# Convolution, Mamba and experts on one core: eight kept images, four pairs held in SBUF up to the loop, and pattern stores and constants at other places

## The chip, the cores and the metric

The kernel runs on one core of one Trainium2 chip. The metric is device time in microseconds (us): the median of three runs, each beginning to end of one execution. A profile of one more execution gives what each engine did and when. Engines are named as in the profile: PE (TensorE), DVE (VectorE), ACT (ScalarE), POOL (GpSimd); SP is the engine that issues most DMAs.

## The reference, cut to what matters

The input is 128 images of 128 channels and 16 x 16 pixels. Three layers follow one another, each added to its input:

```python
def conv_block(x):                      # gn(x) is a group norm over 32 groups
    h = act_quant(bn(x, gamma1, beta1))             # 4 bits
    out = conv3x3(h, weight_quant(w1) * pat1)       # cross pattern, 5 taps
    out = act_quant(bn(out, gamma2, beta2))
    return conv3x3(out, weight_quant(w2) * pat2) + x   # diagonal pattern, 5 taps
v = x + conv_block(gn(x))
t = v.transpose to tokens                           # 256 tokens an image, 128 wide
t = t + mamba(ln(t), fwd) + mamba(ln(t)[::-1], bwd)[::-1]
t = t + moe(ln(t))                                  # top 2 of 8 experts
```

One direction of mamba is a projection to z, x, B, C and dt; a causal convolution of width 4 with silu; softplus of dt; a scan in chunks of 64 tokens (products of decays inside a chunk, states between chunks); a gate silu(z), an RMS norm and a projection back. The layer norm ln is over the 128 channels of a token.

## The kernel before, in words

The images are taken two at a time: 64 pairs, each a tile of 128 channels x 512 pixels, or four tiles of 128 tokens x 128 channels once transposed.

**Setup (0 to 80 us).** SP loads all of x into 64 resident tiles xr (L370, 256 KB each), and behind it the weights of the later layers in 47 small loads (load_weights, L277) and the second convolution's weights w2 (L399). Meanwhile POOL builds two tiles r and c of patterns (L371 to L394), from which the loop makes its decay sums by a matmul; they are stored through POOL's own DMA queue to rows_d and cols_d in memory (L395, L396, 512 KB each). Statistics of each image are taken in four pieces, by DVE (L440) or, for each fourth image, ACT; normed (L417) turns them into a scale and a shift for each image, and into ares and bres (L427, L428), which the residual of the second convolution uses. bst is the table of statistics; one of its columns is set to zero piece by piece (L453). All this is in a pool named setup that is closed afterwards, so its bytes are used again by the first convolution.

**First convolution (80 to 163 us).** For each pair: q = x times scale plus bias on ACT or POOL (L520, L522; four buffers, L516), rounding into a padded image hpad on DVE (L191), five matmuls (L217), and a copy out of PSUM on ACT (L536), with statistics on DVE (L537). The result of the first six pairs stays in SBUF (kept, NKEPT, L559); that of the others is stored to memory (L539).

**Second convolution (169 to 284 us).** fetch (L578) loads a result back, ACT scales it (L582), DVE rounds it (L191), five matmuls; POOL or ACT scale the residual (L612, L610), and DVE adds it (L613). stored (of the pair before) transposes the result in four matmuls (L591), copies it out to a yt tile on ACT (L593, three buffers) and stores it to y_d (L594). At eight places second_weights does a step of work on the loop's weights, through the same two PSUM buffers "cm" as the transposes.

**Order.** Outside the loop the order on each engine is made by an automatic list scheduler: work comes in the order of the program, and work that is ready may go ahead on an engine that is idle. The loop is in a manual order: a table T gives for each step of each part a time within a period of 375 units, in which two pairs are done; the steps are sorted by it and issued so.

**The loop (284 us to the end).** part_a loads yt (for pairs 0 and 1 through POOL's queue, else SP, L713), takes the layer norm (L694 to L705: statistics and their combination on DVE, a power and two small operations on POOL, four scalings on ACT), transposes it on PE (L719) and copies it to uT on ACT (L722). part_c makes the decays for two pairs: dt_ps (L735), its copy dts (L741), a transpose (L743), dtr on DVE (L749), a chain of small DVE and ACT operations to daz (L785), sums r_ps on PE (L793), a store of the cumulative sums through SP (L809), which comes back as e (L953). x_ps (L846) and the rest follow. Before the loop starts, constants() loads three copies each of rows and cols, six loads of 512 KB on SP (L640, L641); in the table they stand after the second step of pair 1's part_a. The first steps of part_a for pairs 0 and 1 go ahead of everything else in the loop.

Of the kernel before, what the change touches and what calls it, by code (L numbers as in the profile page):

```python
# [26 lines left out]
BIG = 1e38  # L27
LNMIN = 2.0 ** -60
G = 4
NKEPT = 6  # L30


@with_exitstack
def kernel(ctx: ExitStack, tc: tile.TileContext, a: dict):
# [308 lines left out]
    with tc.tile_pool(name="w1p", bufs=1) as w1p:  # L343
# [15 lines left out]
        with tc.tile_pool(name="setup1", bufs=1) as setup, tc.tile_pool(  # L359
# [8 lines left out]

            for i in range(NP):
                nc.sync.dma_start(xr[i], x_c[:, 2 * i : 2 * i + 2, :])  # L370
            r = setup.tile([P, NH, 2, 2, P], BF16, name="r0")  # L371
            c = setup.tile([P, 2, 2, 2, 2, P], BF16, name="c0")
            far = setup.tile([HD, 1], BF16, name="far")
            nc.gpsimd.memset(far, -1e30)
            for h in range(NH):
                nc.gpsimd.tensor_copy(
                    r[:, h].rearrange("p d t l -> p (d t l)"), heads[:, h : h + 1].to_broadcast([P, 4 * P])
                )
                nc.gpsimd.tensor_copy(
                    r[0:HD, h].rearrange("p d t (f l) -> p (d t f) l", l=HD),  # L380
                    ident[0:HD, 0:HD].unsqueeze(1).to_broadcast([HD, 2 * 2 * 2, HD]),
                )
            for m in range(2):
                for d in range(2):
                    sign = 1 - 2 * d
                    nc.gpsimd.tensor_copy(
                        c[:, m, d].rearrange("p j f l -> p (j f l)"), triple[:, m : m + 1].to_broadcast([P, 4 * P])
                    )
                    for half in range(2):
                        nc.gpsimd.affine_select(  # L390
                            out=c[0:HD, m, d, :, half, :], in_=far.unsqueeze(2).to_broadcast([HD, 2, P]),
                            pattern=[[0, 2], [sign, P]], compare_op=ALU.is_ge, fill=0.0,
                            base=-sign * HD * half - 1, channel_multiplier=-sign,
                        )  # L394
            nc.gpsimd.dma_start(rows_d, r)  # L395
            nc.gpsimd.dma_start(cols_d, c)  # L396
            load_weights()
            w2 = w1p.tile([P, 9, P], F32, name="w2", tag="w")
            nc.sync.dma_start(w2, a["L0_conv_w2"])  # L399
# [1 line left out]

            bst = setup.tile([P, B, 6], F32, name="bst")
            junk = setup.tile([P, NT], F32, name="junk")

            def tb(name):
                return setup.tile([P, B], F32, name=name)
# [10 lines left out]
            def normed(c):  # L417

                of = slice(cuts[c], cuts[c + 1])
                var_, gm_, dev_, ga_, qv_, dm_ = (t[:, of] for t in (var, gm, dev, ga, qv, dm))  # L420
                nc.vector.reciprocal(ga_, ga_)
                nc.vector.tensor_tensor(dm_, ga_, ga_, ALU.mult)
                nc.vector.tensor_tensor(dm_, dm_, qv_, ALU.mult)
                nc.vector.tensor_scalar(dm_, dm_, -0.5, 1.5, ALU.mult, ALU.add)
                nc.vector.tensor_tensor(ga_, ga_, dm_, ALU.mult)
                nc.vector.scalar_tensor_tensor(shift[:, of], gm_, -1.0, ga_, ALU.mult, ALU.mult)
                nc.vector.tensor_scalar(ares[:, of], ga_, 1.0, SCALE, ALU.add, ALU.mult)  # L427
                nc.vector.tensor_scalar(bres[:, of], shift[:, of], SCALE, None, ALU.mult)  # L428
                nc.vector.tensor_tensor(dev_, dev_, ga_, ALU.mult)
                nc.vector.tensor_tensor(var_, var_, ga_, ALU.mult)  # L430
                nc.vector.tensor_tensor(var_, var_, ga_, ALU.mult)

            for c in range(4):
# [13 lines left out]
                if mine:  # L447

                    picked = slice(mine[0], cuts[c + 1], 4)
                    nc.vector.tensor_scalar(neg[:, picked], bst[:, picked, 1], -1.0 / NT, None, ALU.mult)  # L450
                    nc.vector.tensor_scalar(bst[:, picked, 1], neg[:, picked], -1.0, None, ALU.mult)
                    nc.vector.tensor_scalar(bst[:, picked, 4], neg[:, picked], -1.0, None, ALU.mult)
                    nc.gpsimd.memset(bst[:, picked, 5], 0.0)  # L453
# [29 lines left out]
                if c == 1:  # L483
                    for _ in weights:
                        pass
                if c == 3:
                    normed(c)

# [67 lines left out]
                nc.gpsimd.tensor_scalar(bi2, bet2, NLEV, tmp2, ALU.mult, ALU.add)  # L556


        kepts = ExitStack()  # L559
        keptp = kepts.enter_context(tc.tile_pool(name="keptp", bufs=1, side="right"))  # L560
        kept = {i: keptp.tile([P, 2, NT], F32, name=f"kept{i}") for i in range(min(NKEPT, NP // 4))}

        by_weights(how1, conv1, CROSS)

    def conv2(taps, nq):
        with tc.tile_pool(name="pc", bufs=6) as pc, tc.tile_pool(
# [18 lines left out]
            def stored(i):  # L585
                if i < 0:
                    return
                yt_ps = psw.tile([P, 512], F32, name=f"yt_ps{i}", tag="cm")
                flat = xr[i].rearrange("p b (j l) -> p (b j) l", l=P)
                for t in range(4):  # L590
                    nc.tensor.transpose(yt_ps[:, t * P : (t + 1) * P], flat[:, t, :], ident)  # L591
                yt = pc.tile([P, 4, P], F32, name=f"yt_{i}", tag="yt", bufs=3)
                nc.scalar.activation(yt.rearrange("p t c -> p (t c)"), yt_ps, AF.Copy, scale=1.0 / SCALE)  # L593
                nc.sync.dma_start(y_d[i], yt)  # L594

            for i in range(5):
                fetch(i)
# [2 lines left out]
            for i in range(NP):  # L600
# [12 lines left out]
                behind = nc.vector.scalar_tensor_tensor(xr[i], ps, less, xr[i], ALU.add, ALU.add)  # L613

                stored(i - 1)
                if i % max(NP // 8, 1) == max(NP // 8, 1) - 1:
                    with tc.issue_after(behind.ins):
                        next(weights, None)
            stored(NP - 1)
            for _ in weights:  # L620
                pass

# [39 lines left out]

    yts, uTs, xcs, xts, bcs, ccs, zs, ends_ = {}, {}, {}, {}, {}, {}, {}, {}
    table = ["none"]

    def act(out, in_, func, **more):
# [6 lines left out]

    gps, es, ygs, sqs, rrs, t2s, u2Ts, fps, gbs = {}, {}, {}, {}, {}, {}, {}, {}, {}

    latest = []

    def alone(made):  # L680
        latest[:] = [made.ins]

    def large(made):
        if latest:
            info = mybir.DependencyInfo(mybir.DependencyClass.Sync, mybir.DependencyReason.DATA)
            tc.add_manual_dep(made.ins, latest.pop().name, info, reason="keep apart")

    def layernorm(src, dst, nm):

        s6 = sm.tile([P, 4, 6], F32, name=f"s6{nm}", tag="s6")  # L690
        mv = sm.tile([P, 4, 2], F32, name=f"mv{nm}", tag="mv")
        rstd = sm.tile([P, 4], F32, name=f"rstd{nm}", tag="rstd")
        for t in range(4):
            nc.vector.bn_stats(s6[:, t, :], src[:, t, :])  # L694
        for t in range(4):
            nc.vector.bn_aggr(mv[:, t, :], s6[:, t, :])
        alone(nc.vector.tensor_scalar(rstd, mv[:, :, 1], EPS, None, ALU.add))
        yield
        nmr = sm.tile([P, 4], F32, name=f"nmr{nm}", tag="nmr")
        nc.gpsimd.tensor_tensor(rstd, rstd, mhalf[:, :4], ALU.pow)  # L700
        nc.gpsimd.tensor_tensor(nmr, mv[:, :, 0], rstd, ALU.mult)
        nc.gpsimd.tensor_scalar(nmr, nmr, -1.0, None, ALU.mult)
        yield
        for t in range(4):
            nc.scalar.activation(  # L705
                dst[:, t, :], src[:, t, :], AF.Identity, bias=nmr[:, t : t + 1], scale=rstd[:, t : t + 1]
            )
        yield

    def part_a(i):  # L710

        yt = yts[i] = pr.tile([P, 4, P], F32, name=f"yt{i}", tag="yt", bufs=6)
        (nc.gpsimd if i < 2 else nc.sync).dma_start(yt, y_d[i])  # L713
        yield
        u = pr.tile([P, 4, P], F32, name=f"u{i}", tag="u", bufs=2)
        yield from layernorm(yt, u, f"a{i}")
# [340 lines left out]
    def part_e(i):  # L1057

        u2 = pr.tile([P, 4, P], F32, name=f"u2{i}", tag="u", bufs=2)
        yield from layernorm(t2s[i], u2, f"b{i}")  # L1060
        u2_ps = bank4(f"u2_ps{i}", "o")
        for t in range(4):
            nc.tensor.transpose(u2_ps[:, t, :], u2[:, t, :], ident)  # L1063
# [193 lines left out]

# [28 lines left out]
```

## Time and profile before

| what | us |
|---|---|
| median of 3 runs | 2562.01 (2561.74 to 2562.10) |
| the profiled execution | 2561.65 |
| its span | 2559.9 |
| first matmul of the first convolution | 80.30 |
| first matmul of the second convolution | 168.66 |
| first statistics of the loop (DVE) | 284.08 |

The profiled execution's own time is 1.75 us longer than its span; the sums below are made against that execution. A line of the timeline reads: start, busy time, engine, line and operation, output and inputs by the program's names, shapes, how many instructions are taken together, and in brackets the idle time before the first of them with what ended it. A line of the waits reads: engine and what it waited to do, what it waited for, us in total, how often, the longest.

### The profile page before, as it was taken

Reading aid. Unit: us, or ns where it says so; the run is one execution under the profiler, and the core shown is the slowest. Engines: PE = TensorE matmul, PEld = TensorE weight load, DVE = VectorE, ACT = ScalarE, POOL = GpSimd, SP = SyncE. Lnnn points to the kernel's source line nnn. Section 1 sums busy time; section 2 is a strip of 40 time slices with the busy share of each in tenths; the row PEclk is TensorE's granted clock in tenths of the full one; section 3 lists DMA queues with packets and bytes.
Section 4 is the critical chain, followed back from the end, with each engine's and each line's share of the span. In section 5 each row is a group of like instructions: output and inputs, shape, how many; then the busy total and the mean of one; then the engine's idle time right before and its main releaser. Section 6 shows DMA issues by size and latency. Waiting matters only on the chain.

```text
span 2559.9 us, 49341 instructions
## 1 busy us (share of the span) xinstructions
PE 2420.2 (95%) x15940; PEld 1483.1 (58%) x15940; DVE 2251.0 (88%) x6171; ACT 2174.3 (85%) x4455; POOL 1631.6 (64%) x1692
## 2 busy tenths in 40 slices
PE   0788789999999999999999999999999999999997
PEld 0345355666666666666666666666666666666663
DVE  8887689999999999999999999999999999999883
ACT  5677599888998988889898888898988889898881
POOL 3577025666666667666666766666667666666666
PEclk9999799999999999999999999999999999999998
DMA  9468523334443433444444344433433444444343
GB/s 302 138 233 286 187 68 113 114 118 129 130 120 117 131 121 112 131 132 124 119 125 124 111 124 130 124 123 120 128 118 117 132 132 121 122 124 121 104 126 103
DMA packets 303767, 342.73 MB, mean 134 GB/s; under 512 B 56960, under 2 KB 226944, under 8 KB 303488
## 3 DMA queue, kind: packets, MB, share of 16 engines
q1 hardware_dynamic: 303040, 337.78, 43.1%
q8 instruction: 133, 2.18, 0.3%
q0 software_dynamic: 448, 1.57, 0.2%
q14 instruction: 146, 1.20, 0.2%
HBM read 264.30 MB, written 58.20 MB: 126 GB/s over the span
## 4 chain that ended last, share of the span: by engine, by line
PE 87%; DVE 5%; POOL 2%; ACT 2%; DMA 2%; issue 1%; SPq 0%; DVEq 0%; POOLq 0%; ACTq 0%
PE f_ps L1158 17%; PE x_ps L846 13%; PE y_ps L981 9%; PE z_ps L889 9%; PE o_ps L1041 9%; PE sg L934 5%; PE xt_ps L901 4%; PE y_ps L987 4%; PE g_ps L920 4%; PE cv L217 3%; POOL xr L612 2%; PE n_ps L1014 1%; PE u_ps L1063 1%; PE f_ps L1153 1%; PE u_ps L719 1%
## 5 line engine op out<-in xcount | busy, mean ns | idle before, releaser
L1146 POOL TENSOR_TENSOR gb<-gb,u2T 128x512 f32<-128x512 f32 x512 | 642.6, 1281 | 121.7 <-PE y_ps L987 70.9
L864 DVE SCALAR_TENSOR_TENSOR xc<-x_ps,cw,xc 128x510 f32<-128x510 f32 (+2 forms) x768 | 571.3, 744 | 47.4 <-ACT xc L858 37.8
L997 POOL TENSOR_TENSOR yg<-yg,z 128x512 f32<-128x512 f32 x256 | 326.4, 1280 | 351.0 <-DVE yg L993 155.1
L1158 PE MATMUL f_ps<-gb,ew 128*128 128x512 f32 x1024 | 511.6, 603 | 6.0 <-POOL gb L1146 5.8
L846 PE MATMUL x_ps<-uT,wx 128*128 128x512 f32 x768 | 401.1, 604 | 9.7 <-ACT e L674 3.3
L674 ACT ACTIVATE e<-sg 128x512 f32<-128x512 f32 x512 | 299.6, 592 | 49.7 <-PE sg L934 44.4
L674 ACT ACTIVATE e<-e,ends 128x128 f32<-128x128 f32 x1024 | 324.9, 392 | 0.0
L981 PE MATMUL y_ps<-e,xt 128*64 128x256 f32 x2048 | 317.7, 389 | 0.1
L962 DVE TENSOR_TENSOR e<-e,g_ps 128x1024 f32<-128x1024 f32 x256 | 311.4, 1216 | 5.8 <-ACT e L674 2.7
L864 DVE SCALAR_TENSOR_TENSOR bc<-x_ps,cw,bc 128x510 f32<-128x510 f32 (+2 forms) x384 | 286.6, 746 | 20.5 <-ACT bc L858 4.8
L1158 PEld LDWEIGHTS f_ps<-gb,ew 128*128 128x128 f32 x1024 | 181.2, 192 | 173.5 <-issue 137.2
L889 PE MATMUL z_ps<-uT,wz 128*128 128x512 f32 x512 | 272.2, 613 | 1.6 <-issue 0.8
L858 ACT ACTIVATE xc<-x_ps,cb,cw 128x512 f32<-128x512 f32 x256 | 199.1, 778 | 63.6 <-PE x_ps L846 57.2
L1041 PE MATMUL o_ps<-wo,yg 128*128 128x128 f32 x2048 | 251.3, 276 | 0.2 <-DVE e L967 0.2
L1041 PEld LDWEIGHTS o_ps<-wo,yg 128*128 128x128 f32 x2048 | 240.4, 193 | 11.1 <-DVE g L1118 8.4
L993 DVE SCALAR_TENSOR_TENSOR yg<-xc,dcol,y_ps 128x512 f32<-128x512 f32 x256 | 189.5, 741 | 50.4 <-PE y_ps L987 47.0
L1029 POOL TENSOR_TENSOR rr<-rr,mhalf 128x8 f32<-128x8 f32 x64 | 110.0, 1719 | 161.5 <-DVE g L1120 82.3
L987 PE MATMUL y_ps<-e,xt 128*64 128x128 f32 x2048 | 198.9, 273 | 0.0
L934 PE MATMUL sg<-rows,cols 128*128 128x256 bf16 x1024 | 192.1, 274 | 5.8 <-ACT e L674 2.9
L987 PEld LDWEIGHTS y_ps<-e,xt 128*64 128x64 f32 x2048 | 146.9, 137 | 74.2 <-DVE e L967 0.5
L981 PEld LDWEIGHTS y_ps<-e,xt 128*64 128x64 f32 x2048 | 118.9, 136 | 100.8 <-issue 53.8
L967 DVE TENSOR_TENSOR e<-e,g_ps 128x512 f32<-128x512 f32 x256 | 174.0, 680 | 0.0
(256 smaller groups left out, 4802.0 us busy)
## 6 DMA issues: line engine op xcount, KB each, us to landing
gb<-gd SPq DMA_DIRECT2D x256, 512.0 KB
e<-cum SPq DMA_DIRECT2D x256, 256.0 KB
xr<-in_x SPq DMA_DIRECT2D x64, 256.0 KB
y<-yt SPq DMA_DIRECT2D x64, 256.0 KB
cc<-bc SPq DMA_DIRECT2D x128, 128.0 KB
out<-ob SPq DMA_DIRECT2D x64, 256.0 KB
yt<-y SPq DMA_DIRECT2D x62, 256.0 KB
o<-o SPq DMA_DIRECT2D x58, 256.0 KB
```

What stands on the lines that cost most here:

```text
L674: nc.scalar.activation(out, in_, func, **more)
L846: nc.tensor.matmul(ps, wx[d][:, n * P : (n + 1) * P], uTs[i], start=True, stop=True)
L864: nc.vector.scalar_tensor_tensor(acc[:, :, to], raw[:, :, of], cw[:, d, n, 3 - back : 4 - back], acc[:, :, to], ALU.mult, ALU.add,)
L889: nc.tensor.matmul(ps, wz[:, d, n * P : (n + 1) * P], uTs[i], start=True, stop=True)
L934: nc.tensor.matmul(sg[:, :, of], c_[:, k, d, s, half, :], r_[:, :, d, s, of], start=True, stop=True)
L962: nc.vector.tensor_tensor(e0.rearrange("p h t l -> p h (t l)"), e0.rearrange("p h t l -> p h (t l)"), gps[i, d, k][:, 0:NT].unsqueeze(1).t ...
L981: nc.tensor.matmul(y_ps[64 * q : 64 * q + 64, k, :], xt[:, 2 * k + s0, 64 * h : 64 * h + 64], e0[:, h].rearrange("p t l -> p (t l)"), star ...
L987: nc.tensor.matmul(y_ps[64 * q : 64 * q + 64, k, s1 * P : (s1 + 1) * P], xt[:, 2 * k + s1, 64 * h : 64 * h + 64], e1[:, h, :], start=False ...
L997: large(nc.gpsimd.tensor_tensor(yg, yg, zs[i, d][:, n, :], ALU.mult))
L1041: nc.tensor.matmul(o_ps[:, (2 * j + d) * P : (2 * j + d + 1) * P], ygs[i, d, n][:, t * P : (t + 1) * P], wo[d][:, n, :], start=(n == 0), s ...
L1146: large(nc.gpsimd.tensor_tensor(gb[:, e], gb[:, e], u2Ts[i], ALU.mult))
L1158: nc.tensor.matmul(f_ps, ew[:, e, :], gbs[i, e], start=False, stop=(e == NE - 1))
```

## The change

Eight results of the first convolution stay in SBUF and not six. A new pool, first, lives from before the first convolution to the end of the kernel: it holds yt of pairs 0 to 3 and uT of pairs 0 and 1. The second convolution writes those yt tiles there and doesn't store them, and the loop doesn't load them. For pairs 0 and 1 the layer norm, the transposes and the copy to uT are done inside the second convolution, in five steps each, one step after each pair from pair 32 on (early); in the loop their part_a has empty steps. The function layernorm is moved up and takes the pool as an argument, with its body as before. In setup, the building of the pattern tiles is a function called after the first convolution's weights, and the two stores of them are on SP's queue, emitted after load_weights and w2. The zero column of bst is set once. ares and bres are computed on POOL and not on DVE. The constants are loaded ahead of the loop's first step. No DMA is left on POOL's queue, and the memory set aside for such DMAs (dynamic_dma_scratch_size) is made smaller. What is cut below is marked; the body of patterns() is the loop that is removed, with the tiles' new names.

```diff
@@ constants @@
-NKEPT = 6
+NKEPT = 8
+NFIRST = 4
@@ setup, pattern tiles @@
-            r = setup.tile([P, NH, 2, 2, P], BF16, name="r0")
-            c = setup.tile([P, 2, 2, 2, 2, P], BF16, name="c0")
+            rows0 = setup.tile([P, NH, 2, 2, P], BF16, name="rows0")
+            cols0 = setup.tile([P, 2, 2, 2, 2, P], BF16, name="cols0")
             far = setup.tile([HD, 1], BF16, name="far")
-            nc.gpsimd.memset(far, -1e30)
-            for h in range(NH):
...
-            nc.gpsimd.dma_start(rows_d, r)
-            nc.gpsimd.dma_start(cols_d, c)
+            def patterns():
+                nc.gpsimd.memset(far, -1e30)
+                for h in range(NH):
...
             load_weights()
             w2 = w1p.tile([P, 9, P], F32, name="w2", tag="w")
             nc.sync.dma_start(w2, a["L0_conv_w2"])
@@ setup, statistics @@
+            nc.gpsimd.memset(bst[:, :, 5], 0.0)
...
-                nc.vector.tensor_scalar(ares[:, of], ga_, 1.0, SCALE, ALU.add, ALU.mult)
-                nc.vector.tensor_scalar(bres[:, of], shift[:, of], SCALE, None, ALU.mult)
+                nc.gpsimd.tensor_scalar(ares[:, of], ga_, 1.0, SCALE, ALU.add, ALU.mult)
+                nc.gpsimd.tensor_scalar(bres[:, of], shift[:, of], SCALE, None, ALU.mult)
...
-                    nc.gpsimd.memset(bst[:, picked, 5], 0.0)
...
                 if c == 1:
                     for _ in weights:
                         pass
+                    patterns()
+                    nc.sync.dma_start(rows_d, rows0)
+                    nc.sync.dma_start(cols_d, cols0)
@@ before the first convolution @@
+        first = ctx.enter_context(tc.tile_pool(name="first", bufs=1, side="right"))
+        yts = {i: first.tile([P, 4, P], F32, name=f"yt{i}") for i in range(NFIRST)}
+        uTs = {i: first.tile([P, 4 * P], F32, name=f"uT{i}") for i in range(2)}
@@ second convolution @@
-                yt = pc.tile([P, 4, P], F32, name=f"yt_{i}", tag="yt", bufs=3)
+                yt = yts[i] if i in yts else pc.tile([P, 4, P], F32, name=f"yt_{i}", tag="yt", bufs=3)
                 nc.scalar.activation(yt.rearrange("p t c -> p (t c)"), yt_ps, AF.Copy, scale=1.0 / SCALE)
-                nc.sync.dma_start(y_d[i], yt)
+                if i not in yts:
+                    nc.sync.dma_start(y_d[i], yt)
+
+            def early(i):
+                u = pc.tile([P, 4, P], F32, name=f"u{i}", tag="yt", bufs=3)
+                yield from layernorm(pc, yts[i], u, f"a{i}")
+                u_ps = psw.tile([P, 512], F32, name=f"u_ps{i}", tag="cm")
+                for t in range(4):
+                    nc.tensor.transpose(u_ps[:, t * P : (t + 1) * P], u[:, t, :], ident)
+                yield
+                nc.scalar.copy(uTs[i], u_ps)
+                yield
+
+            early_steps = [step for i in range(2) for step in [early(i)] * 5]
...
                 stored(i - 1)
+                if i >= NP // 2 and early_steps:
+                    next(early_steps.pop(0))
...
             stored(NP - 1)
+            for step in early_steps:
+                next(step)
@@ loop @@
-        yt = yts[i] = pr.tile([P, 4, P], F32, name=f"yt{i}", tag="yt", bufs=6)
-        (nc.gpsimd if i < 2 else nc.sync).dma_start(yt, y_d[i])
-        yield
+        if i >= NFIRST:
+            yts[i] = pr.tile([P, 4, P], F32, name=f"yt{i}", tag="yt", bufs=6)
+            nc.sync.dma_start(yts[i], y_d[i])
+        yield
+        if i < 2:
+            for _ in range(5):
+                yield
+            return
...
-        first = [n for n, (t, *_) in enumerate(steps) if t in [places[0] for places in T["a",]]]
-        for n in first:
-            next(steps[n][2])
-        for n, (t, _, stream) in enumerate(steps):
-            if n not in first:
-                next(stream)
-            if t == T["a",][1][1] and t < PERIOD:
-                constants()
+        constants()
+        for _, _, stream in steps:
+            next(stream)
@@ launch @@
-    nc = bacc.Bacc("TRN2", target_bir_lowering=False, num_devices=1)
+    nc = bacc.Bacc("TRN2", target_bir_lowering=False, num_devices=1, dynamic_dma_scratch_size=1024)
```

More of the change, by code (lines that the diff above doesn't have):

```diff
@@ L370 @@
                 nc.sync.dma_start(xr[i], x_c[:, 2 * i : 2 * i + 2, :])
-            r = setup.tile([P, NH, 2, 2, P], BF16, name="r0")
-            c = setup.tile([P, 2, 2, 2, 2, P], BF16, name="c0")
+            rows0 = setup.tile([P, NH, 2, 2, P], BF16, name="rows0")
+            cols0 = setup.tile([P, 2, 2, 2, 2, P], BF16, name="cols0")
             far = setup.tile([HD, 1], BF16, name="far")
-            nc.gpsimd.memset(far, -1e30)
-            for h in range(NH):
[L376 to L382, printed above, removed]
@@ L383 @@
-            for m in range(2):
-                for d in range(2):
-                    sign = 1 - 2 * d
+            def patterns():
+                nc.gpsimd.memset(far, -1e30)
+                for h in range(NH):
                     nc.gpsimd.tensor_copy(
-                        c[:, m, d].rearrange("p j f l -> p (j f l)"), triple[:, m : m + 1].to_broadcast([P, 4 * P])
+                        rows0[:, h].rearrange("p d t l -> p (d t l)"), heads[:, h : h + 1].to_broadcast([P, 4 * P])
                     )
[L389 to L393, printed above, removed]
-                        )
@@ L395 @@
-            nc.gpsimd.dma_start(rows_d, r)
-            nc.gpsimd.dma_start(cols_d, c)
+                    nc.gpsimd.tensor_copy(
+                        rows0[0:HD, h].rearrange("p d t (f l) -> p (d t f) l", l=HD),
+                        ident[0:HD, 0:HD].unsqueeze(1).to_broadcast([HD, 2 * 2 * 2, HD]),
+                    )
+                for m in range(2):
+                    for d in range(2):
+                        sign = 1 - 2 * d
+                        nc.gpsimd.tensor_copy(
+                            cols0[:, m, d].rearrange("p j f l -> p (j f l)"), triple[:, m : m + 1].to_broadcast([P, 4 * P])
+                        )
+                        for half in range(2):
+                            nc.gpsimd.affine_select(
+                                out=cols0[0:HD, m, d, :, half, :], in_=far.unsqueeze(2).to_broadcast([HD, 2, P]),
+                                pattern=[[0, 2], [sign, P]], compare_op=ALU.is_ge, fill=0.0,
+                                base=-sign * HD * half - 1, channel_multiplier=-sign,
+                            )
@@ L563, with alone, large, layernorm @@
         by_weights(how1, conv1, CROSS)
+    latest = []
+    def alone(made):
+        latest[:] = [made.ins]
+    def large(made):
+        if latest:
+            info = mybir.DependencyInfo(mybir.DependencyClass.Sync, mybir.DependencyReason.DATA)
+            tc.add_manual_dep(made.ins, latest.pop().name, info, reason="keep apart")
+    def layernorm(pool, src, dst, nm):
+        s6 = pool.tile([P, 4, 6], F32, name=f"s6{nm}", tag="s6")
+        mv = pool.tile([P, 4, 2], F32, name=f"mv{nm}", tag="mv")
+        rstd = pool.tile([P, 4], F32, name=f"rstd{nm}", tag="rstd")
+        for t in range(4):
+            nc.vector.bn_stats(s6[:, t, :], src[:, t, :])
+        for t in range(4):
+            nc.vector.bn_aggr(mv[:, t, :], s6[:, t, :])
+        alone(nc.vector.tensor_scalar(rstd, mv[:, :, 1], EPS, None, ALU.add))
+        yield
+        nmr = pool.tile([P, 4], F32, name=f"nmr{nm}", tag="nmr")
+        nc.gpsimd.tensor_tensor(rstd, rstd, mhalf[:, :4], ALU.pow)
+        nc.gpsimd.tensor_tensor(nmr, mv[:, :, 0], rstd, ALU.mult)
+        nc.gpsimd.tensor_scalar(nmr, nmr, -1.0, None, ALU.mult)
+        yield
+        for t in range(4):
+            nc.scalar.activation(
+                dst[:, t, :], src[:, t, :], AF.Identity, bias=nmr[:, t : t + 1], scale=rstd[:, t : t + 1]
+            )
+        yield
     def conv2(taps, nq):
@@ L591, in stored @@
                     nc.tensor.transpose(yt_ps[:, t * P : (t + 1) * P], flat[:, t, :], ident)
-                yt = pc.tile([P, 4, P], F32, name=f"yt_{i}", tag="yt", bufs=3)
+                yt = yts[i] if i in yts else pc.tile([P, 4, P], F32, name=f"yt_{i}", tag="yt", bufs=3)
                 nc.scalar.activation(yt.rearrange("p t c -> p (t c)"), yt_ps, AF.Copy, scale=1.0 / SCALE)
-                nc.sync.dma_start(y_d[i], yt)
+                if i not in yts:
[4 more added lines that the diff above has]
+                u_ps = psw.tile([P, 512], F32, name=f"u_ps{i}", tag="cm")
+                for t in range(4):
+                    nc.tensor.transpose(u_ps[:, t * P : (t + 1) * P], u[:, t, :], ident)
+                yield
+                nc.scalar.copy(uTs[i], u_ps)
+                yield
+            early_steps = [step for i in range(2) for step in [early(i)] * 5]
             for i in range(5):
@@ L661 @@
     NR = NTL * NH * 2
-    yts, uTs, xcs, xts, bcs, ccs, zs, ends_ = {}, {}, {}, {}, {}, {}, {}, {}
+    xcs, xts, bcs, ccs, zs, ends_ = {}, {}, {}, {}, {}, {}
     table = ["none"]
@@ L676, with part_a @@
     gps, es, ygs, sqs, rrs, t2s, u2Ts, fps, gbs = {}, {}, {}, {}, {}, {}, {}, {}, {}
[L678 to L697, printed above, removed]
-        yield
[L699 to L702, printed above, removed]
-        yield
[L704 to L710, printed above, removed]
-        yt = yts[i] = pr.tile([P, 4, P], F32, name=f"yt{i}", tag="yt", bufs=6)
-        (nc.gpsimd if i < 2 else nc.sync).dma_start(yt, y_d[i])
-        yield
+    def part_a(i):
+        if i >= NFIRST:
+            yts[i] = pr.tile([P, 4, P], F32, name=f"yt{i}", tag="yt", bufs=6)
+            nc.sync.dma_start(yts[i], y_d[i])
+        yield
+        if i < 2:
+            for _ in range(5):
+                yield
+            return
         u = pr.tile([P, 4, P], F32, name=f"u{i}", tag="u", bufs=2)
-        yield from layernorm(yt, u, f"a{i}")
+        yield from layernorm(sm, yts[i], u, f"a{i}")
         u_ps = bank4(f"u_ps{i}", "o")
@@ L1059, in part_e @@
         u2 = pr.tile([P, 4, P], F32, name=f"u2{i}", tag="u", bufs=2)
-        yield from layernorm(t2s[i], u2, f"b{i}")
+        yield from layernorm(sm, t2s[i], u2, f"b{i}")
         u2_ps = bank4(f"u2_ps{i}", "o")
```

## The prediction

> **What bounds the kernel now.** I read the page first (busy times, chain of waits), then the timeline at the three places that the change touches: the start of the first convolution, the second convolution, the start of the loop.
>
> ```profile
> span 2559.9 us, 49341 instructions
> PE 2420.2 (95%) x15940; PEld 1483.1 (58%) x15940; DVE 2251.0 (88%) x6171; ACT 2174.3 (85%) x4455; POOL 1631.6 (64%) x1692
> PE 87%; DVE 5%; POOL 2%; ACT 2%; DMA 2%; issue 1%; SPq 0%; DVEq 0%; POOLq 0%; ACTq 0%
> ```
>
> PE is the bound over the whole: 95% busy, 87% of the chain. The idle 5%, some 140 us, lies mostly before the steady loop: setup to 80.3 us, a gap at 162 to 169, a thin start of the loop. The change adds matmuls nowhere and removes none (eight transposes move). So it can only shorten or lengthen those thin places; the loop is issued in a fixed order and PE is full in it from about 350 us, so what its start gains should stay.
>
> Timeline of the start of the first convolution:
>
> ```profile
> 17.94 0.77 POOL L395 DMA_DIRECT2D rows_d<-r  x1
> 19.82 0.56 POOL L396 DMA_DIRECT2D cols_d<-c  x1 [0.17 <-POOL bst L453]
> ...
> 76.48 3.06 ACT L520 ACTIVATE q<-xr,bi,sc 128x256 f32<-128x256 f32 x6 [5.74 <-DVE bi L506]
> 80.30 3.15 PE L217 MATMUL cv<-hpad,wq 128*128 128x512 bf16 x7 [5.94 <-DVE hpad L191]
> 82.37 0.39 SPq L399 DMA_DIRECT2D w<-in_L_conv_w  x1
> ```
>
> The reader sees three facts: the pattern tiles leave SBUF at 18 to 20 us; SP is still issuing weight loads at 82 us, two us after the convolution began; and the convolution waits for DVE's coefficients.
>
> Timeline of the loop's start:
>
> ```profile
> 284.08 0.81 DVE L694 BATCH_NORM_STATS2 s6a<-yt 128x6 f32<-128x128 f32 x4
> 287.16 3.25 ACT L705 ACTIVATE u<-yt,nmra,rstda 128x128 f32<-128x128 f32 x8 [2.24 <-POOL nmra L702]
> 288.58 1.30 SPq L713 DMA_DIRECT2D yt<-y  x2
> 290.93 1.34 PE L735 MATMUL dt_ps<-uT,wdt 128*32 128x128 f32 x16
> 296.78 0.87 DVE L694 BATCH_NORM_STATS2 s6a<-yt 128x6 f32<-128x128 f32 x4 [10.16 <-DMA yt<-y]
> 298.12 0.41 DVE L749 TENSOR_TENSOR dtr<-dt_ps,dtb 128x16 f32<-128x16 f32 x4
> 302.07 1.22 PE L793 MATMUL r_ps<-sums,daz 128*128 128x128 f32 x4 [7.23 <-DVE daz L785]
> ```
>
> L749 heads the chain that releases r_ps, and stands behind pair 2's statistics on DVE, which wait 10.16 us for a load that SP issued behind six constant loads. PE waits 7.23 us for the end of that.
>
> The waits between 165 and 284 us:
>
> ```profile
> DVE xr L613 <- PE cv L217: 19.9, 37, 2.0
> ACT q L582 <- DMA q<-o: 16.2, 18, 1.6
> DVE xr L613 <- POOL xr L612: 5.4, 9, 1.8
> ```
>
> In the second convolution PE and DMA share the bound: 115.5 us for 64 pairs (1.80 each) against 1.54 us of matmul and transposes, at 0.85 DMA share and 285 GB/s.
>
> **What the Trainium skill says.** "DMA: Bandwidth & Descriptors", section "Issuing engines are not separate DMA queues": DMAs of all engines run on the same 16 DMA engines and interleave. The trace agrees: the x loads and the two pattern stores together move some 350 GB/s between 10 and 55 us. "SBUF — State Buffer", section "SBUF: two separate sides": a port pair of DVE and GpSimd is locked for a whole instruction. The trace agrees: a DVE operation of 128x128 (L354) takes 4.44 us from 13.63, and ends at 18.07, 0.08 after POOL's pattern burst at 17.99; a similar one (L81) takes 0.27 when POOL is quiet.
>
> **Loop start: -11.6 us.** Pairs 0 to 3 need no load and pairs 0 and 1 come with uT made. The last transposes of the convolution end at 284.24. dt_ps needs only uT, so it can start at 284.3 in place of 290.93. It takes 0.65 (its later row for 16), the copy to dts ends 0.6 after that, and L743 0.47 later: 286.2. On DVE the memsets L647 end at 284.16; pair 2's statistics, now from SBUF, take 0.81+0.36+0.17 = 1.35 and end by 285.5. L749 then starts at about 286.5, not 298.12: 11.6 earlier. What comes after is late next: the small DVE and ACT steps to daz, 3.9 us as before, all released by L749. The constants now stand first on SP: 3.1 MB at 285.4, at 350 GB/s till about 294.4. The cum store (305.56 before) would be due at 293.9, behind them on the same queue, and costs up to 3 us of delay; its reader e is first needed near 319-11.6, so I cost it at nothing. Without that cover it is 1 to 3 us. Bounds: -8 (constants delay the loop) to -13 (PE's clock, 0.66 granted in 280 to 310, recovers earlier).
>
> **First convolution: +6.0 us.** This is the hidden step. The pattern stores move from POOL's queue at 18 us to SP, where they are emitted behind 64 x loads, the 47 weight loads and w2. SP issues in order. Before, w2 went out at 82.37; the x loads end 3.0 us earlier (1.05 MB of stores no longer among them, at 350 GB/s), so w2 goes at 79.4 and the stores at 80.0 and 80.6. Who waits for them: the first convolution's q buffers (L516) take the place of the setup's closed pool. In the compiled program of before, r lies at bytes 197024 to 201120 of a partition, c at 201120 to 205216, the four q buffers between 197056 and 205248; the first L520 waits for the rows_d store to be complete, and the second pair's for cols_d's. Before, both were met at about 26 us, 50 us ahead of need; after, they are the last to come. Landing: w2 0.59 MB and the store 0.52 MB at 350 GB/s, 3.2 us, and some 2 us fixed, my estimate from the trace: its cum store of 32 KB shows 2.25 us from issue to the load that waits for it. So rows_d is complete at 84.5 to 85. ACT's 0.51 x 2 and DVE's 0.43, with issue gaps, put the first matmul 1.7 later: 86.5 in place of 80.30. Queued behind L520 on ACT are the other q's; POOL's L522 waits likewise. I take +6.0; bounds +4.5 (smaller loads drain faster) and +7.5. That weight loads stood behind x before too is the same in both.
>
> **Setup's engines: 0.** Memsets merged, ares and bres on POOL (8 DVE operations of about 0.1 to 0.2 less), the patterns perhaps built later so that DVE's stalls of 4.2+1.3 us go: all of it makes bi1 earlier by 0 to 5 us, but the hold above ends later than bi1 (76.45), so it is worth nothing while that stands. If the hold is gone, it is 0 to -5. Where the patterns are built later, the same lock may stall DVE there; that too is covered by the hold, up to 6 us.
>
> **Second convolution: 0.** Removed: four y stores (1.05 MB) here, two kept images' store and fetch (0.52 MB each way; the store belongs to the first convolution). At 285 GB/s that is up to 5 us of transfer, but only 16.2 us of ACT's waits over 18 fetches come from DMA, and only two fetches of 58 go: -0.6 by share, -2 at best. Added for pairs 0 and 1: PE 8 x 0.27 = 2.2, DVE 2 x 1.35, ACT 2 x (4 x 0.41 + 0.58) = 4.4, POOL 2 x 1.5 = 3.0. PE idles some 9 us of 110 there, ACT is busy 84 of 110, DVE 77, POOL 70: they fit beside the transfers, except PE's, of which part is paid. The chain has waits: u waits for POOL's pow, u's transposes take a "cm" buffer of two that the y transposes use, and u takes one of three "yt" buffers. Net 0, bounds -3 and +4.
>
> **Sum.** -11.6 + 6.0 + 0 + 0 = -5.6. Against the profiled execution, 2561.65 (span 2559.9 and 1.75 around it): 2556.0. The median of the runs, 2562.01, is 0.36 above it, so 2556.4 there; I write 2556.
>
> **Rivals.**
> B, no hold: the stores go out early on SP (the order of issue outside the loop is made by a scheduler, which could put them among the x loads), or q's addresses are freed otherwise. For it: they are ready early if POOL builds the patterns at once. Against: SP's queue is emitted in that order. Then -11.6 and 0 to -5 of setup: 2545 to 2550, say 2548.
> D, the second convolution gains more than I allow, or the hold is nearer 4: -10, 2552. For it: DMA share of 0.85. Against: PE's waits there are short, 2 us at most.
> C, slower: the early layer norm stalls ACT in the second convolution. POOL runs ahead through L612 from 170.78 at 0.617 each; if pair 0's pow stands behind 59 of them, it comes at 207.2, and nmr at 208.8. If ACT reaches u at about 198.4, it stands 10.4 us, with all later q's behind it, so hpad and PE wait. With both pairs' chains conv2 grows by 8 to 12: total +2.4 to +6.4, 2566 in the middle. It ends slower from 5.6 us of stall on. Against: u's buffer follows pair 31's yt, which ACT makes at about 226, long after POOL's pow.
>
> **Chances.** About 0.2%, 5.1 us, is what a measurement here can tell from no change. A (forecast, 2553 to 2559) 0.55: it straddles -5.1, so 0.31 faster, 0.24 same. B 0.17 and D 0.13, faster. C 0.15: 0.10 slower, 0.05 same. Together 0.61, 0.29, 0.10. The range 2546 to 2565 leaves out a third of B and half of C, 0.13.
>
> **What would show it.** Hold: the pattern stores on SP's queue after w2 at about 80, and ACT's first q waiting for them, first matmul at 86 to 87. Wrong if it is at 80 or earlier. Loop start: L749 within 2 to 3 us of the last transposes and no wait for yt. Conv2: first to last matmul still 115 to 116 us; C if ACT's u shows a long wait for POOL.

## The result, and the profile after

The changed kernel takes 2557.66 us, the median of 20 runs (2554.65 to 2561.57); the kernel before, in 20 runs beside them, 2562.29 (2559.89 to 2566.29). The ratio is 0.9981, with a 95% interval of 0.9974 to 0.9988: 4.6 us less, by the medians. The profiled execution of the changed kernel took 2554.94 us and has a span of 2553.1, so it lies at the fast end of its runs, 6.7 below the profiled execution of before (6.8 by the spans).

The views here and below show the lines that matter; lines between them are left out. The page of the changed kernel: span, busy times, and the chain that ended last by engine.

```profile
span 2553.1 us, 49290 instructions
PE 2415.3 (95%) x15940; PEld 1479.9 (58%) x15940; DVE 2253.2 (88%) x6163; ACT 2173.0 (85%) x4455; POOL 1629.3 (64%) x1694
PE 88%; DMA 4%; DVE 3%; ACT 2%; issue 1%; SPq 1%; POOL 1%; POOLq 0%; ACTq 0%; DVEq 0%
```

PE has as many matmuls as before and is as busy. What has changed is in the small shares: DMA is 4% of the chain in place of 2%, and DVE 3% in place of 5%. Two percent are some 50 us, far more than the change can have cost: it is the path through setup that is another. Before, the chain up to the first matmul went in large part through DVE's statistics; now it goes through the loads of x, SP's issuing of the weight loads one after the other, and the landing of a pattern store. The timeline of the changed kernel from 79 us on shows where the two paths meet.

```profile
79.03 0.67 SPq L401 DMA_DIRECT2D w<-in_L_conv_w  x1
79.74 0.43 SPq L489 DMA_DIRECT2D rows_d<-rows  x1
80.21 0.43 SPq L490 DMA_DIRECT2D cols_d<-cols  x1
85.72 3.23 ACT L525 ACTIVATE q<-xr,bi,sc 128x256 f32<-128x256 f32 x6 [13.64 <-DMA rows_d<-rows]
85.75 0.16 DVE L211 TENSOR_SCALAR less<-less_ps 128x1 f32<-128x1 f32 x1 [8.13 <-DMA rows_d<-rows]
87.06 7.28 POOL L527 TENSOR_SCALAR q<-xr,sc,bi 128x256 f32<-128x256 f32 x11 [10.59 <-DMA cols_d<-cols]
87.33 12.85 PE L218 MATMUL cv<-hpad,wq 128*128 128x512 bf16 x47 [11.41 <-DVE hpad L192]
```

The reader sees the hold of the prediction's second step: the pattern stores are the last of SP's queue, ACT's first q waits for the first of them to land, POOL's for the second, and the first matmul is at 87.33 and not at 80.30.

The loop's start in the changed kernel, from its timeline:

```profile
292.12 0.86 DVE L589 BATCH_NORM_STATS2 s6a<-yt 128x6 f32<-128x128 f32 x4
292.91 0.65 PE L766 MATMUL dt_ps<-uT,wdt 128*32 128x128 f32 x16
293.61 1.04 POOL L595 TENSOR_TENSOR rstda<-rstda,mhalf 128x4 f32<-128x4 f32 x1 [44.83 <-issue]
294.31 0.42 DVE L780 TENSOR_TENSOR dtr<-dt_ps,dtb 128x16 f32<-128x16 f32 x4
298.44 0.71 PE L824 MATMUL r_ps<-sums,daz 128*128 128x128 f32 x4 [3.31 <-DVE daz L816]
```

dt_ps (290.93 before, under L735) follows the last transposes of the convolution at once, and pair 2's statistics need no load. The wait of 10.16 us for a load is gone.

From each trace I took when certain instructions start; the differences of these, stage by stage, add up to what the profiled execution gained in span. A group of transposes counts from the start of its last one.

| stage | before | after | difference | predicted |
|---|---|---|---|---|
| to the first matmul of the first convolution | 80.3 | 87.3 | +7.0 | +6.0 |
| from there to the first matmul of the second | 88.4 | 87.4 | -1.0 | 0 |
| from there to the last group of transposes | 115.3 | 118.0 | +2.7 | 0 (-3 to +4) |
| from there to dtr | 14.15 | 1.60 | -12.55 | -11.6 |
| from dtr to the 25th x_ps | 52.3 | 50.9 | -1.4 | in the bound of -13 |
| from there to the last o_ps | 2167.76 | 2167.76 | 0.0 | 0 |
| to the end | 41.7 | 40.1 | -1.6 | 0 |

### The profile page after: what moved, and what is told of

It reads as the page before. It is cut to its first block, busy times and chain, and to the rows that moved or that the text cites. A ratio compares the mean times of both kernels' runs of the same rounds, so it can differ in the third digit from the quotient of the medians.

```text
span 2553.1 us, 49290 instructions
## 1 busy us (share of the span) xinstructions
PE 2415.3 (95%) x15940; PEld 1479.9 (58%) x15940; DVE 2253.2 (88%) x6163; ACT 2173.0 (85%) x4455; POOL 1629.3 (64%) x1694
## 4 chain that ended last, share of the span: by engine, by line
PE 88%; DMA 4%; DVE 3%; ACT 2%; issue 1%; SPq 1%; POOL 1%; POOLq 0%; ACTq 0%; DVEq 0%
PE f_ps L1189 17%; PE x_ps L877 13%; PE y_ps L1012 10%; PE z_ps L920 9%; PE o_ps L1072 9%; PE sg L965 5%; PE xt_ps L932 4%; PE y_ps L1018 4%; PE g_ps L951 4%; PE cv L218 4%; DMA xr<-in_x 2%; PE n_ps L1045 1%; PE u_ps L1094 1%; PE f_ps L1184 1%; PE u_ps L750 1%
## 5 line engine op out<-in xcount | busy, mean ns | idle before, releaser
L218 PE MATMUL cv<-hpad,wq 128*128 128x512 bf16 x640 | 161.7, 396 | 19.5 <-DVE hpad L192 19.4
```

## The experiments

The open questions were four: whether the late start is the hold on q's bytes or something else; what lies under the hold (the wait of q, the scaled input of the first convolution, until the pattern stores have left its bytes); which part of the loop's start is the load and which the layer norm; and whether the second convolution pays for the early steps.

**The hold alone.** In e1_apart the two pattern tiles take bytes of the setup pool that the q buffers don't use; the stores stay where they are.

```diff
-            rows0 = setup.tile([P, NH, 2, 2, P], BF16, name="rows0")
-            cols0 = setup.tile([P, 2, 2, 2, 2, P], BF16, name="cols0")
-            far = setup.tile([HD, 1], BF16, name="far")
...
                 tb(n) for n in ("mean", "var", "dm", "gm", "dev", "qv", "ga", "neg", "shift")
             )
+            rows0 = setup.tile([P, NH, 2, 2, P], BF16, name="rows0")
+            cols0 = setup.tile([P, 2, 2, 2, 2, P], BF16, name="cols0")
+            far = setup.tile([HD, 1], BF16, name="far")
```

> The changed kernel, with the two pattern tiles at bytes that the first convolution's q buffers do not use (their order in the setup pool); the stores stay last on SP. If q waits for the stores because it lies on their tiles (my step), ACT's first q starts right behind bi1 (77.6 us), the first matmul comes at about 81.4 in place of 87.33, and the whole is about 5.9 us faster than the changed kernel: 2552, ratio to before 0.996. If the late start has another cause (SP's queue, weights, DMA traffic), the first matmul stays at 87 and the time at 2557 to 2558.

Measured: 2550.47 us (5 runs), ratio to the kernel before 0.9958, interval 0.9944 to 0.9972. Its timeline at the start of the first convolution:

```profile
77.34 0.29 DVE L511 TENSOR_SCALAR bi<-bi,b 128x128 f32<-128x128 f32 x1
77.71 3.06 ACT L525 ACTIVATE q<-xr,bi,sc 128x256 f32<-128x256 f32 x6 [5.61 <-DVE bi L511]
...
80.75 0.43 SPq L489 DMA_DIRECT2D rows_d<-rows  x1
81.23 0.43 SPq L490 DMA_DIRECT2D cols_d<-cols  x1
81.82 8.44 PE L218 MATMUL cv<-hpad,wq 128*128 128x512 bf16 x27 [6.15 <-DVE hpad L192]
```

The stores go out as late as in the changed kernel, even a little later, and the convolution starts beside them. So neither SP's queue nor the traffic held it; the shared bytes did. 5.5 us of the late start are this wait. The other 1.5 (81.8 against 80.3) are bi1, the biases of q and the last result of setup (`bi` in the views), which is ready 1.2 later than before, and 0.35 on the way from it to the matmul.

**The order alone.** e2_stores_early leaves the tiles in place and puts the stores ahead of the weight loads.

```diff
+            patterns()
+            nc.sync.dma_start(rows_d, rows0)
+            nc.sync.dma_start(cols_d, cols0)
             load_weights()
...
-                    patterns()
-                    nc.sync.dma_start(rows_d, rows0)
-                    nc.sync.dma_start(cols_d, cols0)
```

> The changed kernel, with the pattern stores on SP behind the x loads but ahead of the 47 weight loads. My step: stores land near 58 us, q waits for bi1 alone, first matmul at about 81.4, total 2552, as in e1_apart. Rival: the weight loads, one us later each, or the traffic hold the convolution and the start stays near 87.

Measured: 2549.28 us (4 runs), ratio 0.995 (0.9933 to 0.9966); stores issued at 51.92 and 52.67, first matmul at 81.34. Either edit takes the hold away. Their difference of 1.2 us lies within their intervals.

**What the hold hid.** In the changed kernel one DVE operation of setup, the scaling of the mask grp, takes 7.84 us (4.44 before). e4_grp_pool gives it to POOL; e5_apart_grp does that and takes the hold away too.

```diff
-        nc.vector.tensor_scalar(grp, grp, 0.25, None, ALU.mult)
+        nc.gpsimd.tensor_scalar(grp, grp, 0.25, None, ALU.mult)
```

> The changed kernel, with the scaling of grp (one DVE operation that takes 7.84 us there beside POOL's pattern burst) on POOL. If the hold decides the start, bi1 gets up to 7 us earlier (about 71) and the first matmul stays at 87.3: no change, 2557 to 2558. If DVE's work in setup decides, the first matmul comes at 80 to 82 and the total falls by 5 to 7.

> Both edits. If the hold hides a setup that is bound by DVE, taking both away adds up: bi1 at 70 to 72, first matmul at 74 to 76, total 2545 to 2547, ratio 0.994. If x's loads, ACT or the weights bound setup, the first matmul stays at about 81 as in e1_apart, 2552.

Measured: e4_grp_pool 2556.28 us (20 runs), ratio 0.9981 (0.9974 to 0.9988), the same as the changed kernel's; e5_apart_grp 2544.92 us (4 runs), 0.9938 (0.9921 to 0.9954). The timeline of e4_grp_pool:

```profile
72.45 0.28 DVE L511 TENSOR_SCALAR bi<-bi,b 128x128 f32<-128x128 f32 x1
80.30 0.43 SPq L489 DMA_DIRECT2D rows_d<-rows  x1
86.43 3.18 ACT L525 ACTIVATE q<-xr,bi,sc 128x256 f32<-128x256 f32 x6 [19.23 <-DMA rows_d<-rows]
88.04 2.29 PE L218 MATMUL cv<-hpad,wq 128*128 128x512 bf16 x5 [17.48 <-DVE hpad L192]
```

and that of e5_apart_grp:

```profile
72.46 0.29 DVE L511 TENSOR_SCALAR bi<-bi,b 128x128 f32<-128x128 f32 x1
72.83 3.06 ACT L525 ACTIVATE q<-xr,bi,sc 128x256 f32<-128x256 f32 x6 [5.62 <-DVE bi L511]
76.93 13.27 PE L218 MATMUL cv<-hpad,wq 128*128 128x512 bf16 x48 [6.13 <-DVE hpad L192]
```

The same 4.9 us that DVE gives back (bi1 done at 72.7 and not 77.6) are worth nothing under the hold, where q's wait only grows from 13.64 to 19.23, and all 4.9 at the first matmul without it (76.93 against 81.82).

**The same operation in the kernel before**, where no hold stands (the same edit):

> The kernel before, with the scaling of grp on POOL and nothing else. There q has no late store to wait for. If DVE's work bounds setup, the 4.44 us of that operation come off: bi1 72.5 in place of 76.4, first matmul 76.4 in place of 80.3, total 4 us less, ratio 0.9985. If x's loads (last issue 53.9) or ACT bound it, the start stays at 80 and the total is the same.

Measured: bi1 at 73.1, first matmul at 76.99, 3.3 earlier and not 3.9, so DVE bounded setup there. The total was 2559.50 us (13 runs), ratio 0.9993 (0.9984 to 1.0001): the time isn't told from no change, though setup is shorter in the profile. The 1.5 us by the medians are less than setup gained; the interval reaches to 4.

Without grp's scaling on DVE bi1 is done at 73.1 here and at 72.7 in e4_grp_pool. So the change's other edits in setup, ares and bres on POOL and the merged memset among them, are worth some 0.4 us on bi1.

**Load or layer norm.** e3_no_early holds yt for pairs 0 to 3, but does the layer norm of pairs 0 and 1 in the loop.

```diff
-        uTs = {i: first.tile([P, 4 * P], F32, name=f"uT{i}") for i in range(2)}
+        uTs = {}
...
-            early_steps = [step for i in range(2) for step in [early(i)] * 5]
+            early_steps = []
...
-        if i < 2:
-            for _ in range(5):
-                yield
-            return
```

> The changed kernel without the early steps: pairs 0 and 1 keep yt in SBUF, their layer norm is done in the loop again. If the layer norm chain was on the path (my step: 6.6 us of the 11.6), dtr starts some 8 to 9 us behind the last transposes in place of 1.6, the second convolution is 1 to 3 us shorter, and the total is 4 to 6 us above the changed kernel, 2561 to 2563. Rival: the load alone was the wait, and the chain hides beside other work: dtr within 4 us of the last transposes, total 2555 to 2557.

Measured: 2561.07 us (12 runs), ratio 0.9998 (0.9989 to 1.0006). Its timeline:

```profile
293.17 0.87 DVE L589 BATCH_NORM_STATS2 s6a<-yt 128x6 f32<-128x128 f32 x4
293.82 3.26 ACT L600 ACTIVATE u<-yt,nmra,rstda 128x128 f32<-128x128 f32 x8 [1.62 <-POOL nmra L597]
297.61 1.34 PE L762 MATMUL dt_ps<-uT,wdt 128*32 128x128 f32 x16
299.84 0.42 DVE L776 TENSOR_TENSOR dtr<-dt_ps,dtb 128x16 f32<-128x16 f32 x4 [4.17 <-PE dt_ps L770]
```

Pair 2's statistics are early now, from SBUF, and dtr waits for dt_ps and for no load. It starts 8.6 us behind the last transposes: of the 12.55 us, 5.6 are the load's and 7.0 the layer norm chain's. With the hold (first matmul at 88.04 here) and without the early steps nothing of the gain is left, and the kernel is as fast as before.

**Kept images.** e7_kept6 sets NKEPT back.

```diff
-NKEPT = 8
+NKEPT = 6
```

> The changed kernel with six kept images. My step: two stores and two fetches of 256 KB more are worth 0.6 to 2 us at most: 2558 to 2560, first convolution 0.7 to 0.9 longer (its store traffic), second the same within its spread. Rival: the two kept images shape the second convolution's start and are worth over 3 us.

Measured: 2555.82 us (15 runs), ratio 0.998 (0.9972 to 0.9988). The changed kernel's own ratio is 0.9981: the two kept images bring nothing that can be measured, and the expectation of up to 2 us missed. The first convolution was not longer without them either (80.9 us to its last statistics, 81.4 and 82.1 in the two profiles with them).

**What spreads.** The kernel before once more, and the changed one once more:

> The kernel before, profiled once more, to see which stages repeat. If the spread of a few us between executions sits in one stage, that is the second convolution (last transposes minus first matmul 115.3 us in the first profile; it was 115.2 to 119.5 in the five profiles with early steps), and setup, first convolution, the start of the loop (14.15 us from last transposes to dtr) and the loop repeat within 0.3. If the second convolution too repeats within 0.3 us, the lengths with early steps are their cost and not noise.

> The changed kernel once more. My reading: first matmul at 86 to 88 (the store's landing some 6 us behind its issue at 79.7), dtr 1.6 behind the last transposes, second convolution 117 to 119. If the second convolution is at 115 to 116, the early steps' cost is not told from the spread.

Measured: the kernel before has its first matmul at 80.25, dtr 14.02 behind the last transposes, and a second convolution of 116.3; the changed one 87.67, 1.59, and 118.4. The first matmul and dtr repeat within 0.4 us, the second convolution within 1.0 and 0.4. The expectation that all but one stage repeat within 0.3 missed: from dtr to the 25th x_ps the kernel before took 54.1 in place of 52.3, the loop's later part was 1.4 shorter, and the last stage 40.8 in place of 41.7. The 25th x_ps is a poor mark, for what one side of it gains the other loses: from dtr to the last o_ps the two profiles of the kernel before have 2220.1 and 2220.5 us, those of the changed one 2218.7 and 2219.1. Over all thirteen profiles the last stage lies between 39.1 and 41.9 for kernels that don't differ in it. The -1.6 of the table's last line is therefore not put down to the change.

**The early steps' price.** In the changed kernel PE has the transposes of u right behind ACT's making of it. The waits of the changed kernel from 239 to 256 us:

```profile
PEld u_ps L642 <- ACT u L600: 3.4, 4, 1.8
DVE xr L666 <- PE u_ps L642: 2.9, 2, 1.8
PE u_ps L642 <- ACT u L600: 2.2, 2, 1.4
```

PE stands twice for u, with convolution matmuls behind it. e8_spaced, made from e5_apart_grp, leaves two more steps between the two; e10_spaced_again is the same kernel.

```diff
                 yield from layernorm(pc, yts[i], u, f"a{i}")
+                yield
+                yield
                 u_ps = psw.tile([P, 512], F32, name=f"u_ps{i}", tag="cm")
...
-            early_steps = [step for i in range(2) for step in [early(i)] * 5]
+            early_steps = [step for i in range(2) for step in [early(i)] * 7]
```

> e5_apart_grp with two empty steps between ACT's u and PE's transposes of it, so that PE doesn't stand before transposes whose input ACT has not made (0.7 and 1.2 us of waits, twice, beside 2.2 us of work). If those waits are the early steps' cost, the second convolution is 1 to 2.5 us shorter than in e5_apart_grp (116.8) and the total 2543; if the cost is ACT's and DVE's time, no change, 2545.

> The same kernel as e8_spaced, for its time and for the length of its second convolution. If spacing the transposes takes the early steps' cost away, the second convolution is at 114.5 to 115.8 again (before: 115.3 and 116.3; early steps unspaced: 115.2 to 119.5, mean 117.5) and the total 2543 to 2545, ratio 0.993 to 0.994; if e8_spaced was a lucky draw, it is at 117 to 118.

Measured: 2544.56 us (4 runs, ratio 0.9937, 0.9918 to 0.9957) and 2542.78 (5 runs, 0.9933, 0.992 to 0.9947). The timeline of the second:

```profile
230.26 1.64 ACT L600 ACTIVATE u<-yt,nmra,rstda 128x128 f32<-128x128 f32 x4
233.72 0.42 PEld L644 LDWEIGHTS u_ps<-ident,u 128*128 128x128 f32 x4 [0.70 <-ACT yt L633]
233.73 0.66 PE L644 MATMUL u_ps<-ident,u 128*128 128x128 f32 x4 [0.47 <-ACT yt L633]
```

The four transposes now run as one group of 0.66 us, with u long done, and PE waits only for a free buffer (1.0 us for both groups together). The second convolution (first matmul to last group of transposes) lasts 114.6 and 115.3 us. By kind: without early steps 115.3, 115.7, 116.3 and 116.6 (mean 116.0, the two profiles of before, e3_no_early, e9_before_grp); with early steps as written 115.2 to 119.5, mean 117.6 over seven profiles; spaced 115.0. So by these means the early steps cost about 1.6 us as written, and no cost is seen when they are spaced. The means are of few profiles with a wide spread. In all seven with the steps as written PE's matmuls wait 1.7 to 2.2 us for u, in e1_apart too, whose second convolution took only 115.2: something else moves this stage as well, and no run tells what. The whole time of e8_spaced and e10_spaced_again isn't told from that of e5_apart_grp, and of e5_apart_grp itself there is one profile of the stage, 116.8. All three beat both kernels: they are 0.6 to 0.7% under the kernel before, where the changed kernel is 0.2% under it.

## Why the prediction came out right, and where it was off

The forecast was 2556, the sum -5.6; the profiled execution shows -6.7 and the medians -4.6. Case A held, with both of its main terms, the hold and the loop's start. That the sum is so near is in part luck. By the means of both profiles of each kernel the terms were off by +1.2 (first convolution's start), -0.4 (its length), +2.4 (second convolution), -0.9 and -2.0 (loop's start and what follows), and these nearly cancel.

**Loop start, -11.6: measured -12.55, and 1.4 more behind it.** The order of events is the one described: dt_ps at once, statistics from SBUF, then dtr, 1.6 behind the last transposes. The chain from dt_ps to dtr was sized too long. The prediction gave it 2.2 us, with the copy's 0.6 and the transpose's 0.47 as they were in the kernel before, where PE's granted clock was 0.50 from 290 to 300 us. In the changed kernel the clock is still 1.00 from 292.91 to 294.31, the copy ends 0.33 after dt_ps, the transpose takes 0.33, and the chain 1.40. Pair 2's statistics begin before the last group of transposes (292.12, against 292.35), so they hold nothing up.

The prediction's bound of -13 was for a clock that recovers earlier, and it does. In the 25 us after the last transposes it was granted 0.73 in the changed kernel and 0.59 before, as these windows of the two show (the columns are us, busy time and count of each engine, clock, DMA share and GB/s; the changed kernel first).

```profile
292.70:317.70 25.00, 17.57 (x59) 7.75 (x58) 20.79 (x62) 14.54 (x27) 2.93 (x6) 0.73 0.55 188
```

```profile
284.00:309.00 25.00, 13.78 (x52) 7.33 (x50) 11.74 (x62) 10.64 (x24) 5.88 (x12) 0.59 0.46 170
```

The -1.4 from dtr on is found again in the second profiles, up to the last o_ps. It is not the early steps', for e3_no_early has 2219.1 there too. Whether it is the clock's, no run shows. The constants on SP ahead of the cum store cost nothing visible in it.

**First convolution, +6.0: measured +7.0.** The mechanism was right: e1_apart moves nothing but addresses and gets 5.5 back. Mis-sized was the landing. I let the store share the engines with w2 alone, gave it 5 us, and had it complete at 84.5 to 85. The two stores go out half a microsecond apart, and w2, rows_d and cols_d move together: 1.6 MB, at some 370 GB/s between 82 and 86, is 4.4 us. A line of the changed kernel's chain (start, us, what) shows the landing, at 85.6:

```profile
79.74 5.88 DMA rows_d<-rows
```

The trace of before held a warning that the prediction did not use: there, beside the loads of x, the same store took 6.8 us from issue to landing. The prediction cites the Trainium skill, "DMA: Bandwidth & Descriptors", section "Issuing engines are not separate DMA queues": DMAs of different issuing engines interleave on the same 16 DMA engines. I had used it for the x loads. Here all three transfers are of SP's queue, of which the section does not speak; that they share the engines too is what this trace shows.

**Setup's engines, 0: right, for the reason given, but the sign beneath was wrong.** I had costed DVE's work as up to 5 us lighter. It got heavier: bi1 was done at 77.6 and not 76.4. The other edits gave some 0.4 us, but DVE reached the scaling of grp 2.5 us earlier than before and was blocked there until POOL's pattern burst ended, for 7.84 us in place of 4.44:

```profile
11.14 7.84 DVE L355 TENSOR_SCALAR grp<-grp 128x128 f32<-128x128 f32 x1
```

The scheduler built the patterns as early as before (8.7 to 18.9 us) although the program calls for them later. e4_grp_pool and e5_apart_grp show both halves: hidden under the hold, 4.9 us without it. So rival B, no hold, would not have come to 2548 by a faster setup; e1_apart and e2_stores_early are that case, and they measured 2550.5 and 2549.3. One reading of the prediction was wrong: L81's 0.27 us were not beside a quiet POOL. POOL was in a memset then (2.93 to 3.56).

**Second convolution, 0 with bounds -3 and +4: measured +2.7 in one profile, +1.6 in the mean of all profiles with the steps as written.** The stores and fetches that went brought nothing that is seen (e3_no_early, without them and without the early steps, 115.7; the kernel before 115.3 and 116.3), and the early steps had a cost. Rival C named the wrong engine: POOL's pow stood behind 59 of its residual scalings and came at 213.66, as reckoned (207.2, in a stage that began 6 us later), and ACT's u only at 241.52, as I had argued against C. The stall that the traces show is PE's, for u. My list of waits had u waiting for POOL and for buffers, but not PE waiting for u. With the means of both profiles of each kernel the stages up to the 25th x_ps come to 7.2 - 0.4 + 2.4 - 12.5 - 2.0 = -5.3; the rest of the loop is +0.6 and the last stage -1.6. The medians' difference is -4.6, with an interval from -6.7 to -3.1, and the last stage's spread of 2.8 is part of what lies between.

## What to carry to other kernels

A store that is moved to the end of a queue moves the moment when its source's bytes come free: look up which later buffer takes those bytes, and whether it is the first thing that the next stage needs. A stage that hides behind a wait must still be measured; when the wait goes, it is the next bound, and here it was worth 4.9 us beside the wait's 5.5. Where a step is put into a running pipeline, give the in-order engine that consumes a result a distance from its producer: the same eight transposes cost about 1.6 us in the mean or nothing that could be seen.

## What the runs showed of the hardware

The block of a DVE operation by POOL lasted over many POOL instructions, not one. grp's 128x128 scaling took 7.84 us while POOL issued its copies (CAST in the views) and selects back to back from 8.75 to 18.9, against 0.27 for a like operation (L81 of the kernel before) beside a POOL memset. It took 4.44 in the kernel before, 6.68 in e2_stores_early and 7.87 in e1_apart. In e2_stores_early it ended at 18.01, inside a memset of POOL (17.86 to 18.26) and before the burst's end at 18.9; in the kernel before at 18.07, when POOL had just turned to issuing a DMA (17.94). Operations of another kind in the same stretch were not held: thirteen bn_stats took 4.51 us beside the burst in e4_grp_pool, and three took 1.06 right after it in the changed kernel.

The Trainium skill, "SBUF — State Buffer", section "SBUF: two separate sides", gives the lock for the length of one instruction; these traces show that a run of POOL instructions without gaps can keep it for much longer. It need not: a second scaling of L81's, at 9.91 in the same burst of the kernel before, was done after 1.56 us, with POOL still busy. What decides between the two no run shows.
